# Four graph-attention layers on one Trainium2 core: the adjacency turned by DMA out of two bf16 scratch matrices in DRAM, in place of transposes on TensorE

## The chip, the cores and the metric

The kernel runs on one core of one Trainium2 chip. The metric is the device time of one execution in microseconds (us). Most executions of one kernel agree within 0.3%. The engines are called as the profile calls them: PE is TensorE (PEld its weight loads), DVE is VectorE, ACT is ScalarE, POOL is GpSimd and SP is SyncE. In the traces of this case ScalarE and PE are seen to take their instructions in the order in which the program lists them: in the changed kernel ScalarE stands 9.97 us at one instruction with a ready one behind it, and PE 5.88 us (both are shown below).

## The reference, cut to what matters

Sixteen batches, each a graph of 1024 nodes with 256 features, go through four attention layers one after the other. All four layers read the same adjacency matrix of the batch.

```python
x = normal(16, 1024, 256)                      # f32
a = bernoulli(1/256, (16, 1024, 1024))
a = a | swapaxes(a, -1, -2) | eye(1024)        # symmetric, with ones on the diagonal
adj = a.astype(int32)
# four times, with a different attention each time:
h = maximum(layernorm(x), 0)
x = x + attention_l(h, adj, W_l, a_l)          # [...]
```

The adjacency of one batch is 4 MB of int32. It is **symmetric** in these inputs.

## The kernel before

The kernel keeps a `mask` of uint8 in SBUF for each batch, with the neighbour on the partitions. The attention weights of a layer are a row (one value for each node, the same on all partitions), times or against a column value, times the mask. `load(b)` makes the mask: it fetches 128 rows of the adjacency (the DMA turns int32 into bf16), sums squares of them on ScalarE as a check that every entry is 0 or 1, turns the tile with eight TensorE transposes into PSUM, and casts it to uint8 on ScalarE.

```python
    def load(b):
        # [...] x_b, mask
        def fetch(i):
            fetched[i] = adjs.tile([P, N], BF, name="adj_i")          # adjs has 3 buffers
            nc.gpsimd.dma_start(fetched[i], adj[b, ts(i, P), :])       # L106
        for i in range(AHEAD):                                         # AHEAD = 2
            fetch(i)
        yield
        for i in range(NI):                                            # 8 tiles
            if i + AHEAD < NI:
                fetch(i + AHEAD)
            adj_i = fetched.pop(i)
            every = wide.tile([P, N], BF, name="wide")
            nc.scalar.activation(every, adj_i, AF.Square, bias=minus_half,
                                 accum_out=squares[:, b, i : i + 1])   # L117
            turned = psum.tile([P, NI, P], BF, name="misc", bufs=3)
            for j in range(NI):
                nc.tensor.transpose(turned[:, j, :], adj_i[:, ts(j, P)], ident_b)   # L122
            nc.scalar.copy(masks[b][:, :, ts(i, P)], turned)           # L123
            yield
```

Two streams of batches (even and odd) run interleaved. While layer 3 of batch b runs, `load(b + 2)` advances by one step for each half head:

```python
        coming = load(b + 2) if b + 2 < B else iter(())
        # [...] layers 0, 1 and 2
        yield from weigh3(0)                       # first row copy and weights of layer 3
        for n in range(H * NH):                    # 8 half heads
            yield from weigh3(n + 1)
            # [...] 8 matmuls accT <- V3, w        (L427)
            nc.scalar.copy(sums, accT)             # L431
            next(coming, None)                     # one step of load(b + 2)
```

The order in which this code is written is not the order in which the engines run it. A scheduler, working from its own idea of how long each instruction and each transfer takes, moves instructions forward on every engine. An instruction marked with `tc.keep_in_program_order` is exempt: it stays behind everything that was written before it for its engine. I call such an instruction *pinned*.

## Time and profile before

| | before |
|---|---|
| time, median of 3 runs | 3268.11 us (3267.7 to 3269.8) |
| span of the profiled execution, clock | 3267.0 us, 0.984 |
| PE busy, idle | 3075.9 us, 191.1 us |
| share of PE in the chain that ended last | 70% |

The prediction shows the lines for PE's fullness, for the transposes and for the start of layer 3. Two more views matter. The first is the page's part 4: the engines' shares of the chain of work that ended last, followed backwards from the last instruction.

```profile
PE 70%; DVE 18%; POOL 6%; issue 2%; ACT 2%; DMA 1%; SPq 0%; ACTq 0%; POOLq 0%
```

The second is the table of waits. A line names the engine, the tile and line that waited, after the arrow what it waited for, then us in total, how often, and the longest.

```profile
POOL adj_i L106 <- ACT sums L431: 214.6, 51, 14.8
DVE weights L262 <- ACT row L258: 84.6, 28, 8.6
```

The chain is mostly matmuls that follow one another.

### The profile page before, as it was taken

What the parts mean: (1) busy time and instruction counts of PE and PEld (TensorE: products, weight loads), DVE (VectorE), ACT (ScalarE), POOL (GpSimd) and SP (SyncE); (2) the same over time, 40 slices, a digit from 0 to 9 for tenths busy, and PEclk for the clock granted to TensorE, in tenths of its full rate; (3) what the DMA queues carried; (4) which work ended last, traced back from release to release, by engine and by line L of the source; (5) the groups of instructions that cost most, each with busy time, mean ns of one, the idle gap of its engine ahead of it and who ended that gap; (6) DMA issues with size and microseconds to landing.
All of it is one profiled execution on the core that took longest, in us unless ns stands there. A gap on an engine that the chain in (4) does not pass through costs nothing.

```text
span 3267.0 us, 38466 instructions
## 1 busy us (share of the span) xinstructions
PE 3075.9 (94%) x13702; PEld 2129.5 (65%) x13702; DVE 2546.5 (78%) x6140; ACT 969.5 (30%) x2081; POOL 1086.2 (33%) x1286
## 2 busy tenths in 40 slices
PE   6999999999999999999999999999999999999987
PEld 5776766657666676666766667676676766767562
DVE  5778787777877778877788877888778787787767
ACT  3423323232332323323233232322323223232121
POOL 1323424233242332423334233342323423233242
PEclk8999999999999999999999999999999999999998
DMA  4101101011010111100111010110101101000000
GB/s 118 27 4 17 33 12 41 7 16 30 14 39 7 17 29 17 36 10 13 30 17 36 10 17 28 15 36 13 39 4 17 33 13 40 4 14 13 1 13 14
DMA packets 55190, 73.18 MB, mean 22 GB/s; under 512 B 4048, under 2 KB 37968, under 8 KB 54992
## 3 DMA queue, kind: packets, MB, share of 16 engines
q0 software_dynamic: 18432, 33.56, 7.0%
q1 hardware_dynamic: 36560, 37.10, 3.6%
q8 instruction: 110, 1.80, 0.2%
q14 instruction: 88, 0.72, 0.1%
HBM read 87.43 MB, written 16.78 MB: 32 GB/s over the span
## 4 chain that ended last, share of the span: by engine, by line
PE 70%; DVE 18%; POOL 6%; issue 2%; ACT 2%; DMA 1%; SPq 0%; ACTq 0%; POOLq 0%
PE acc L346 31%; PE acc L427 22%; PE projected L242 11%; DVE weights L262 8%; PE misc L235 2%; PE misc L254 2%; POOL x_b L282 2%; DVE centered L227 2%; DVE stats L222 2%; POOL rstd L213 1%; PE misc L122 1%; DVE above L280 1%; DVE above L281 1%; DMA adj_i<-in_adj_dram 1%; POOL y L407 1%
## 5 line engine op out<-in xcount | busy, mean ns | idle before, releaser
L346 PE MATMUL acc<-V,weights 128*128 128x257 f32 x6144 | 1440.8, 384 | 8.4 <-DVE weights L262 7.0
L346 PEld LDWEIGHTS acc<-V,weights 128*128 128x128 f32 x6144 | 1139.5, 191 | 205.0 <-DVE weights L262 38.6
L427 PE MATMUL acc<-weights,V 128*65 128x512 f32 x2048 | 913.2, 594 | 0.3 <-DVE weights L262 0.3
L262 DVE SCALAR_TENSOR_TENSOR weights<-row,ex,mask 128x512 f32<-128x512 f32 x1024 | 744.9, 776 | 36.7 <-ACT row L258 36.7
L262 DVE SCALAR_TENSOR_TENSOR weights<-row,V,mask 128x512 f32<-128x512 f32 x768 | 593.4, 815 | 49.3 <-ACT row L258 47.9
L213 POOL TENSOR_TENSOR rstd<-rstd,minus_half 128x2 f32<-128x2 f32 (+1 forms) x320 | 330.2, 1034 | 883.3 <-DVE rstd L212 834.9
L427 PEld LDWEIGHTS acc<-weights,V 128*65 128x65 f32 x2048 | 279.4, 138 | 499.4 <-issue 477.2
L242 PE MATMUL projected<-W,hT 128*128 128x259 f32 (+1 forms) x2048 | 522.3, 397 | 40.8 <-DVE V L297 24.9
L242 PEld LDWEIGHTS projected<-W,hT 128*128 128x128 f32 x2048 | 388.1, 195 | 137.0 <-DVE V L297 37.5
L282 POOL TENSOR_TENSOR x_b<-x_b,above 128x256 f32<-128x256 f32 x256 | 222.1, 868 | 478.9 <-DVE above L281 436.6
L278 ACT ACTIVATE below<-acc,inv 128x256 f32<-128x256 f32 x256 | 121.0, 473 | 657.1 <-DVE inv L271 463.5
L222 DVE BATCH_NORM_STATS2 stats<-x_b 128x6 f32<-128x256 f32 x512 | 209.3, 415 | 126.0 <-POOL x_b L282 121.1
L235 PE MATMUL misc<-ident,centered 128*128 128x128 f32 x1024 | 168.5, 281 | 75.7 <-DVE centered L227 70.3
L237 ACT COPY hT<-misc 128x512 f32<-128x512 f32 x256 | 147.2, 588 | 299.6 <-PE misc L235 298.9
L227 DVE TENSOR_SCALAR centered<-x_b,mv 128x256 f32<-128x256 f32 x512 | 229.6, 451 | 4.7
L431 ACT COPY sums<-acc 65x512 f32<-65x512 f32 x128 | 74.1, 579 | 513.9 <-PE acc L427 512.4
L235 PEld LDWEIGHTS misc<-ident,centered 128*128 128x128 f32 x1024 | 120.8, 143 | 128.2 <-DVE centered L227 107.9
L258 ACT COPY row<-misc 128x512 f32<-128x512 f32 x224 | 129.8, 587 | 196.2 <-PE misc L254 196.0
L106 POOL DMA_DIRECT2D adj_i<-in_adj_dram x128 | 77.6, 606 | 287.4 <-ACT sums L431 214.6
L280 DVE TENSOR_SCALAR above<-acc,inv 128x256 f32<-128x256 f32 x256 | 122.8, 480 | 61.8 <-ACT below L278 60.9
L392 POOL TENSOR_TENSOR y<-y,bias 128x512 f32<-128x512 f32 x64 | 90.5, 1414 | 234.2 <-DVE y L439 215.9
L293 ACT ACTIVATE V<-projected,rstd 128x3 f32<-128x3 f32 x384 | 99.3, 263 | 228.0 <-PE projected L242 227.4
(70 smaller groups left out, 2311.4 us busy)
## 6 DMA issues: line engine op xcount, KB each, us to landing
adj_i<-in_adj_dram POOLq DMA_DIRECT2D x128, 256.0 KB, 3.9
x_b<-in_x_dram SPq DMA_DIRECT2D x16, 1024.0 KB, 7.9
out_dram<-y SPq DMA_DIRECT2D x32, 512.0 KB, 3.6
W<-in_L_gnn_W_dram SPq DMA_DIRECT2D x3, 256.0 KB, 3.6
a_b<-in_L_gnn_a_dram SPq DMA_DIRECT2D x3, 256.0 KB, 7.4
a_b<-in_L_gnn_a_src_dram SPq DMA_DIRECT2D x1, 640.0 KB, 8.4
a_b<-in_L_gnn_a_dst_dram SPq DMA_DIRECT2D x1, 640.0 KB, 10.2
W<-in_L_gnn_W_dram SPq DMA_DIRECT2D x2, 128.0 KB, 9.4
```

Source lines behind the costliest of these rows:

```text
L213: nc.gpsimd.tensor_tensor(r, r, minus_half.to_broadcast([P, n]), op=ALU.pow)
L222: nc.vector.bn_stats(stats, xb[:, 2 * pair + n, :])
L227: nc.vector.tensor_scalar(centered[:, n, :], xb[:, 2 * pair + n, :], mv[:, n, 0:1], 0.0, op0=ALU.subtract, op1=ALU.max,)
L235: nc.tensor.transpose(turned[:, k, ts(n, P)], centered[:, n, ts(k, P)], ident)
L237: nc.scalar.copy(hT, turned)
L242: nc.tensor.matmul(projected, hT[:, k, ts(n, P)], W[l][:, k, :], start=(k == 0), stop=(k == NK - 1),)
L258: nc.scalar.copy(r, turned)
L262: nc.vector.scalar_tensor_tensor(w[:, j, :], r, c(j), mask[:, j, ts(half, HALF)], op0=op, op1=ALU.mult)
L280: nc.vector.tensor_scalar(above, acc[:, :D], inv, 0.0, op0=ALU.mult, op1=ALU.max)
L282: nc.gpsimd.tensor_add(xi, xi, above)
L346: nc.tensor.matmul(acc, w[:, j, ts(i % NG, P)], V[:, j, : D + 1], start=(j == 0), stop=(j == NI - 1),)
L427: nc.tensor.matmul(accT, V3[:, j, h, :], w[:, j, :], start=(j == 0), stop=(j == NI - 1))
```

## The change

The intent is to take the 1024-element transposes of the adjacency off the full engine. For all batches but the first two, GpSimd issues four DMAs that copy the matrix, narrowed to bf16, into one of two scratch matrices in DRAM. SyncE then issues DMAs that read 128 columns of it and turn them on the way into SBUF. ScalarE casts the turned tile to the mask straight from SBUF. The four casting DMAs are pinned; the square and the mask cast, which read the turned tiles, are not.

```diff
+    dram = ctx.enter_context(tc.tile_pool(name="dram", bufs=1, space=bass.MemoryType.DRAM))
 [...]
+    narrows = [dram.tile([N, N], BF, name=f"narrow{n}") for n in range(2)]
 
     def load(b: int):
 [...]
+        by_dma = b >= 2
         fetched = {}
 
+        if by_dma:
+            for q in range(4):
+                rows = ts(q, N // 4)
+                cast = nc.gpsimd.dma_start(narrows[b % 2][rows, :], adj[b, rows, :])
+                tc.keep_in_program_order(cast)
+
         def fetch(i: int):
             fetched[i] = adjs.tile([P, N], BF, name="adj_i")
-            nc.gpsimd.dma_start(fetched[i], adj[b, ts(i, P), :])
+            if by_dma:
+                nc.sync.dma_start_transpose(fetched[i], narrows[b % 2][:, ts(i, P)])
+            else:
+                nc.gpsimd.dma_start(fetched[i], adj[b, ts(i, P), :])
 [...]
-            turned = psum.tile([P, NI, P], BF, name="misc", bufs=3)
-            for j in range(NI):
-                nc.tensor.transpose(turned[:, j, :], adj_i[:, ts(j, P)], ident_b)
-            nc.scalar.copy(masks[b][:, :, ts(i, P)], turned)
+            if by_dma:
+                nc.scalar.copy(masks[b][:, i, :], adj_i)
+            else:
+                # [...] as before
```

More of the change, by code (lines that the diff above doesn't have):

```diff
@@ L119, in load @@
             )
-            turned = psum.tile([P, NI, P], BF, name="misc", bufs=3)
-            for j in range(NI):
-                nc.tensor.transpose(turned[:, j, :], adj_i[:, ts(j, P)], ident_b)
-            nc.scalar.copy(masks[b][:, :, ts(i, P)], turned)
+            if by_dma:
+                nc.scalar.copy(masks[b][:, i, :], adj_i)
+            else:
+                turned = psum.tile([P, NI, P], BF, name="misc", bufs=3)
+                for j in range(NI):
+                    nc.tensor.transpose(turned[:, j, :], adj_i[:, ts(j, P)], ident_b)
+                nc.scalar.copy(masks[b][:, :, ts(i, P)], turned)
             yield
```

## The prediction

> **What bounds the kernel now.** I read the page's first two parts first: which engine is full, and whether it is full everywhere.
>
> ```profile
> PE 3075.9 (94%) x13702; PEld 2129.5 (65%) x13702; DVE 2546.5 (78%) x6140; ACT 969.5 (30%) x2081; POOL 1086.2 (33%) x1286
> PE   6999999999999999999999999999999999999987
> DMA  4101101011010111100111010110101101000000
> ```
>
> TensorE is busy in every slice; ScalarE and the DMA engines have most of their time free. So PE work that goes away is worth its full length, and work moved to ScalarE or the DMA engines costs nothing, as long as nobody on PE's path has to wait for it. Next come the groups of the adjacency (busy us, mean ns of one), and the chain of waits in a stretch where a tile is turned (start, us, what).
>
> ```profile
> L122 PE MATMUL misc<-ident_b,adj_i 128*128 128x128 bf16 x1024 | 80.9, 225 | 29.3 <-DVE ident_b L84 15.3 <-DMA adj_i<-in_adj_dram 12.3 <-ACT mask L123 1.2
> L123 ACT CAST mask<-misc 128x1024 uint8<-128x1024 bf16 x128 | 128.9, 1009 | 6.8 <-PE misc L122 6.8
> ...
> 1648.93 5.15 PE acc L427 x12
> 1654.08 0.45 PE misc L122 x8
> 1654.53 3.52 PE acc L346 x16
> ```
>
> One transpose lasts 225 ns but they are pipelined: eight of them, one adjacency tile, hold the chain for 0.45 us, between matmuls that follow without a gap. That is the price of a tile, not 8 x 225 ns. ScalarE waits only 6.8 us in all before the mask casts: the transposes it now depends on are never late.
>
> Last, what happens where layer 3 of a batch starts, since there the changed kernel does its casts. Timelines of three engines around 1600 us:
>
> ```profile
> 1599.48 0.73 POOL L321 TENSOR_TENSOR x_b<-x_b,beta 128x256 f32<-128x256 f32 x1
> ...
> 1605.97 1.08 ACT L237 COPY hT<-misc 128x512 f32<-128x512 f32 x2 [3.64 <-PE misc L235]
> 1609.24 0.58 ACT L258 COPY row<-misc 128x512 f32<-128x512 f32 x1
> ...
> 1612.64 1.92 PE L242 MATMUL projected<-W,hT 128*128 128x259 f32 x8
> 1614.40 7.03 PE L427 MATMUL acc<-weights,V 128*65 128x512 f32 x16
> ```
>
> From the last x_b + beta on GpSimd to the first layer-3 matmul are 14.9 us here. Over the 14 batches that load another, the timelines show two kinds: 14.9 us for odd batches, 11.2 us for even ones. The row copy on ScalarE must end before VectorE can make the weights (0.74 us each here), and those before L427.
>
> **What the Trainium skill says.** "DMA: Bandwidth & Descriptors", section "Anatomy of one DMA", fits a GpSimd-issued DMA as about 2.0 us fixed plus bytes at 436 GB/s. The trace agrees on the fixed part: an adjacency tile reads 512 KB and lands in 3.9 us. Its rate is lower: queue 0 wrote 33.56 MB in 7.0% of 3267 us = 229 us, so 147 GB/s written, 294 GB/s read.
>
> ```profile
> q0 software_dynamic: 18432, 33.56, 7.0%
> adj_i<-in_adj_dram POOLq DMA_DIRECT2D x128, 256.0 KB, 3.9
> ```
>
> The same page, "Latency and other measured facts", gives a DMA transpose an effective 261 GB/s for a non-contiguous case; "VectorE: DVE Perf Modes", section "The three transpose paths", gives 1309 ns for one 128x128 bf16 block. No transpose DMA is in this trace, so these stay unchecked. My estimate for one 128x1024 tile, from both: some 2 us fixed, 1 us of bytes, and the descriptors for eight blocks on top: 4.5 us to landing (3 to 10), and 2 us between tiles issued back to back. "TensorE: Matmul & The Clock Gate", Part 1, says that TensorE falls to half its clock after an idle window of about 3.4 us. The trace agrees: after PE had waited 2.0 us at 1522.8, the stretch that follows ran at a granted 0.58.
>
> ```profile
> 1505.00:1511.00 6.00, 6.00 (x15) 1.92 (x14) 6.00 (x10) 0.76 (x2) 2.38 (x2) 1.00 0.00 0
> 1522.70:1526.60 3.90, 3.80 (x7) 1.36 (x8) 3.87 (x21) 0.59 (x1) 2.54 (x4) 0.58 0.02 4
> ```
>
> 3.9 us at 0.58 instead of 1.00 lose 3.9 x 0.42 = 1.6 us.
>
> **The change part by part.**
>
> *Removed from PE.* 14 batches x 8 tiles = 112 of 128 groups of transposes: 112 x 0.45 = 50 us, all on the chain. With them go most of the waits they cause: PE's transposes of the sums wait 11.6 us for the mask cast, and GpSimd stands in front of tile fetches whose buffer isn't free. I put 12 us on these. Gain: 62 us.
>
> *ScalarE.* The mask cast now reads SBUF instead of PSUM, the same 1024 elements. The square over the same tile takes 1145 ns from SBUF, so I expect 1.0 to 1.15 us against 1009 ns: 0 to 16 us on an engine that is 30% busy. Nothing.
>
> *GpSimd.* 56 casts of a quarter (1 MB read, 0.5 MB written) replace 112 fetches at 606 ns. Nothing, and it no longer waits for buffers.
>
> *The new path: cast, transpose, square.* This is where I expect the cost. The instruction order of the changed kernel, which can be read without running it, has in every batch the same pattern. On GpSimd the four casts stand right behind the last x_b + beta, with two tiles' V products between them. On ScalarE the first square of the new tile stands behind the hT copies of the last pair, **ahead of** the first row copy of layer 3. ScalarE takes its instructions in order. The square needs the first transpose, which needs all four casts. Before, the tile had been fetched long ahead; now the scheduler puts some 8 us between cast and square.
>
> Worked for an odd batch on the clock above. Casts issue from 1600.2 (end of x_b + beta) to about 1604. 4 MB at 294 GB/s are 14.3 us; with about 2 us of start and completion they end near 1617. The first transpose lands 4.5 us later, at 1621. ScalarE stands at the square from 1607. After it come the square (1.33 us with its accumulator read), one or two ex and h copies (0.75), the row copy (0.58), and one weights instruction (0.74): L427 starts at about 1621 + 3.4 = 1624.4 instead of 1614.4, 10 us late. PE can't fill this: in its order L427 stands before the other stream's matmuls. For an even batch the room is 11.2 instead of 14.9 us: 13.6 us late. Mean 11.8.
>
> After a gap of such length PE runs some 4 us at about half clock: 1.6 us. Later in the batch three casts into the mask follow soon after the square that frees their transpose's buffer (three buffers): ScalarE stands again for about 4.5 - 3 us each time. PE has queued work then, so I count 2 us per batch. Sum: 11.8 + 1.6 + 2 = 15.4 us, x 14 = 216 us.
>
> *Net.* 3268 - 62 + 216 = 3422. Large descriptors could make the casts somewhat faster than the fetches' 294 GB/s, so I go down a little: 3400.
>
> **The rivals.** (1) *The DMA path is hidden and only the 62 us show: 3206.* For it: the DMA engines are nearly idle, a batch takes 200 us, and eight tiles at 4.5 us need 36. Against it: what counts is not the rate but the distance between the casts and the first square in program order, and that is 8 us where at least 10 of cast and 3 of transpose have to fit, even at the best rate. With 10 us of cast and 3 of transpose, L427 is still 3 to 7 us late: 14 x (5 + 3) - 62 = +50, 3318. (2) *The transposes are slow, 10 us each and one after the other.* Nothing in this trace speaks against it. Then tile 0 comes 5.5 us later, and the second and third, which stand before the second row copy, hold ScalarE again by some 5 to 10 us: 14 x 28 - 62 = +330, 3600. (3) *The casts from DRAM to DRAM are slower than the fetches,* because they write to DRAM: 20 instead of 14.3 us adds 14 x 6 = 80 us: 3480. (4) *The new order of instructions happens to be better or worse elsewhere.* The scheduler rearranges around it; the pattern is the same in all batches, so a few us per batch either way, +-40.
>
> **Range and chances.** Rival 1's milder form (3318) and rival 3 to halfway rival 2 (3480 to 3560) set the range: 3290 to 3560. Faster by over 2% means below 3203, more than the whole gain of 62 us without any cost: 0.04. Within 2%, up to 3333, needs less than 9 us lost per batch: 0.16. Slower: 0.80.
>
> **What would show it.** Right: the chain of waits has no L122 group in later batches; ScalarE's square idles for 9 to 20 us once per batch, released by the DMA of adj_i; the first L427 of each batch stands about 25 us behind the last x_b + beta, and the window behind it has a granted clock near 0.6; the issues list gives casts of about 14 us for a batch and transposes of 3 to 6 us to landing; busy time of PE falls by about 50 us while its idle time rises by 150 or more. Wrong: if the squares wait little, my clock of the casts is off (they issue earlier or move faster than 294 GB/s); if ScalarE waits as long as I say and the time hardly grows, PE had other work in its queue; if the waits lie at the mask casts and not at the square, it is the transposes that are slow.

## More of the kernel before

GpSimd stands for 214.6 us in front of fetches of adjacency tiles, and nobody is seen to suffer from it: in the whole run ScalarE's squares wait 8.2 us for fetched tiles. VectorE waits 84.6 us for the row copies on ScalarE.

## The result, and the profile after

| | before | after |
|---|---|---|
| time, median (range), 4 runs each in the same rounds | 3268.29 us (3267.7 to 3269.8) | 3392.74 us (3389.9 to 3400.36) |
| span of the profiled execution, clock | 3267.0 us, 0.984 | 3388.3 us, 0.973 |
| PE busy, idle | 3075.9, 191.1 us | 3045.9, 342.4 us |

The ratio is 1.0379, with a 95% interval of 1.0363 to 1.0395. Ratios in this document are the mean time of one kernel's fast runs over the mean of the other's fast runs of the same rounds, so they are not quite the ratio of the medians beside them. The results are correct. The changed kernel is 3.8% slower.

The added lines of code shift the line numbers. In the changed kernel the square is L129, the mask cast from SBUF L133, the row copy L273 (L258 before), the transposes that make a row L269 (L254), the weights L277 (L262), and the layer-3 matmul L442 (L427).

From the page of the changed kernel, parts 1, 2 and 4: busy time of each engine, busy tenths of PE and DMA in 40 slices, and the engines' shares of the last chain.

```profile
PE 3045.9 (90%) x12806; PEld 2091.9 (62%) x12806; DVE 2551.7 (75%) x6140; ACT 969.7 (29%) x2081; POOL 1048.9 (31%) x1230
...
PE   6989899898998989989899898998999888999987
...
DMA  4110210202002020020201102020020211200000
...
PE 44%; DVE 37%; POOL 8%; DMA 6%; ACT 3%; issue 2%; SPq 0%; ACTq 0%; POOLq 0%
```

PE has lost 30 us of work and gained 151 us of idle time (342.4 against 191.1). Its row of solid nines has broken into eights and nines: the loss is spread over the whole run. DMA, 1% of the chain before, now has 6%.

The page's parts 3 and 6 say how the new transfers went: the queue of the casting DMAs (packets, MB, share of 16 engines' time), then the issues with their size and the median us from issue to landing.

```profile
q0 software_dynamic: 4096, 33.56, 5.1%
...
narrow<-in_adj_dram POOLq DMA_DIRECT2D x56, 512.0 KB, 8.1
...
adj_i<-narrow SPq DMA_TRANSPOSE x112, 3.5
```

A transposing DMA lands after 3.5 us in the median (3.1 to 5.4 over all). The transfers are not slow. The waits tell who stood for them:

```profile
DVE weights L277 <- ACT row L273: 244.7, 27, 16.1
...
ACT wide L129 <- DMA adj_i<-narrow: 159.2, 14, 13.2
...
PE misc L269 <- ACT ex L328: 111.5, 14, 10.5
...
ACT mask L133 <- DMA adj_i<-narrow: 53.5, 50, 3.3
```

The second line carries the result: ScalarE's square waits 14 times, once for each batch loaded in the new way, 11.4 us on average. The waits of VectorE for ScalarE's row copies have grown from 84.6 to 244.7 us with it, and PE waits 14 times for `ex`, which ScalarE makes too. The chain of waits in one such place shows the path (start, us, what):

```profile
1660.09 0.72 POOL x_b L336
1660.81 0.55 POOL narrow L110
...
1664.65 9.38 DMA narrow<-in_adj_dram
...
1674.17 3.43 DMA adj_i<-narrow
...
1677.63 0.02 ACT wide L129
...
1679.60 0.47 PE misc L269
1680.08 3.41 PE projected L257 x8
1683.48 6.87 PE acc L442 x16
```

This is the same batch whose start of layer 3 the prediction shows at 1600 us. The casts are issued right behind the last x_b + beta, the last of the four lands at 1674.05, the first turned tile 3.4 us after its issue, and only then does ScalarE go on. The timelines of ScalarE and PE in the same stretch show what stood behind the square (start, us, engine, line, operation; in brackets the idle time before it and what ended it):

```profile
1666.58 1.08 ACT L252 COPY hT<-misc 128x512 f32<-128x512 f32 x2 [3.64 <-PE misc L250]
1677.63 1.15 ACT L129 ACTIVATE wide<-adj_i,minus_half 128x1024 bf16<-128x1024 bf16 x1 [9.97 <-DMA adj_i<-narrow]
...
1679.79 0.60 ACT L273 COPY row<-misc 128x512 f32<-128x512 f32 x1
1680.25 2.97 ACT L133 CAST mask<-adj_i 128x1024 uint8<-128x1024 bf16 x3
...
1679.08 1.00 PE L269 MATMUL misc<-ident,ex 128*128 128x128 f32 x2 [5.88 <-ACT ex L328]
...
1683.32 7.03 PE L442 MATMUL acc<-weights,V 128*65 128x512 f32 x16
```

ScalarE stood for 9.97 us with the `ex` and the row copy queued behind the square, although PE had finished the projection that this `ex` reads at 1669.3. From the start of the last x_b + beta (1660.09) to the first layer-3 matmul (1683.32) are 23.2 us; before, in the same batch, 14.9 us. PE stood for 5.88 us, from 1673.2 to 1679.08, at the transposes of `ex` that make a row, with eight projection matmuls (`projected`) queued behind them; the last part of this wait and the work after it fall into a window at half the clock, in which the eight took 3.61 us in place of 1.92. In the chain these eight, and not the row copy or the weights, stand last before the layer-3 matmul. Columns of the windows: start and end, length, busy time of PE, PEld, DVE, ACT and POOL, granted clock, DMA share, GB/s.

```profile
1677.00:1683.00 6.00, 3.87 (x10) 2.92 (x11) 2.58 (x4) 5.37 (x10) 1.49 (x4) 0.50 0.50 93
```

I read the start of layer 3 off the timelines in all batches, and split the time into this *stage* (last x_b + beta to first layer-3 matmul) and the rest of the batch:

| | before | after |
|---|---|---|
| stage, even batches (start to start) | 11.2 us | 22.5 to 23.7 us |
| stage, odd batches | 14.9 us | 22.5 to 23.7 us |
| stages of the 14 batches that load another, sum of the increase | | +142 us |
| rest of these batches, sum | 2618 us | 2599 us, so -19 us |
| start of the run and its tail | | -5 us |

The sum, +118 us, is the difference of the two spans (+121) to within what such reading gives. The stages are longer by 10.15 us each, and the rest is shorter by only 1.3 us. PE's own waits give nearly the same: it waits 111.5 us for `ex`, 8.0 us per batch, where the kernel before has no such wait on PE, and the half clock from there to the layer-3 matmul costs 1.9 us per batch by the trace.

### The profile page after: what moved, and what is told of

The parts are those of the page before. It is cut to its first block, busy times and chain, and to the rows that moved or that the text cites. A ratio compares the mean times of both kernels' runs of the same rounds, so it can differ in the third digit from the quotient of the medians.

```text
span 3388.3 us, 36818 instructions
## 1 busy us (share of the span) xinstructions
PE 3045.9 (90%) x12806; PEld 2091.9 (62%) x12806; DVE 2551.7 (75%) x6140; ACT 969.7 (29%) x2081; POOL 1048.9 (31%) x1230
## 2 busy tenths in 40 slices
DMA packets 159121, 102.45 MB, mean 30 GB/s; under 512 B 121425, under 2 KB 155345, under 8 KB 158033
## 3 DMA queue, kind: packets, MB, share of 16 engines
q1 hardware_dynamic: 154832, 66.47, 8.0%
## 4 chain that ended last, share of the span: by engine, by line
PE 44%; DVE 37%; POOL 8%; DMA 6%; ACT 3%; issue 2%; SPq 0%; ACTq 0%; POOLq 0%
PE acc L361 20%; DVE weights L277 18%; PE acc L442 14%; PE projected L257 7%; DMA narrow<-in_adj_dram 4%; DVE centered L242 3%; DVE stats L237 2%; POOL x_b L297 2%; POOL y L407 2%; DVE above L295 2%; DMA adj_i<-narrow 2%; PE misc L250 2%; DVE y L408 1%; DVE V L312 1%; DVE above L296 1%
## 5 line engine op out<-in xcount | busy, mean ns | idle before, releaser
L361 PE MATMUL acc<-V,weights 128*128 128x257 f32 x6144 | 1423.1, 381 | 7.5 <-DVE weights L277 5.3
L442 PE MATMUL acc<-weights,V 128*65 128x512 f32 x2048 | 922.5, 599 | 0.3 <-DVE weights L277 0.3
L277 DVE SCALAR_TENSOR_TENSOR weights<-row,ex,mask 128x512 f32<-128x512 f32 x1024 | 745.4, 775 | 199.2 <-ACT row L273 199.2
L277 DVE SCALAR_TENSOR_TENSOR weights<-row,V,mask 128x512 f32<-128x512 f32 x768 | 582.7, 801 | 47.6 <-ACT row L273 45.5
L442 PEld LDWEIGHTS acc<-weights,V 128*65 128x65 f32 x2048 | 283.1, 140 | 507.4 <-issue 488.0
L257 PE MATMUL projected<-W,hT 128*128 128x259 f32 (+1 forms) x2048 | 543.0, 409 | 52.1 <-DVE V L312 24.5
L257 PEld LDWEIGHTS projected<-W,hT 128*128 128x128 f32 x2048 | 397.5, 201 | 164.3 <-ACT hT L252 53.7
L242 DVE TENSOR_SCALAR centered<-x_b,mv 128x256 f32<-128x256 f32 x512 | 247.0, 485 | 4.3
L250 PEld LDWEIGHTS misc<-ident,centered 128*128 128x128 f32 x1024 | 120.4, 142 | 180.7 <-DVE centered L242 134.8
L129 ACT ACTIVATE wide<-adj_i,minus_half 128x1024 bf16<-128x1024 bf16 x128 | 146.1, 1144 | 168.8 <-DMA adj_i<-narrow 159.2
L269 PE MATMUL misc<-ident,ex 128*128 128x128 f32 x512 | 89.2, 283 | 112.1 <-ACT ex L328 111.5
L273 ACT COPY row<-misc 128x512 f32<-128x512 f32 x224 | 129.9, 587 | 144.2 <-PE misc L269 144.1
```

Source lines behind the costliest of these rows:

```text
L242: nc.vector.tensor_scalar(centered[:, n, :], xb[:, 2 * pair + n, :], mv[:, n, 0:1], 0.0, op0=ALU.subtract, op1=ALU.max,)
L250: nc.tensor.transpose(turned[:, k, ts(n, P)], centered[:, n, ts(k, P)], ident)
L257: nc.tensor.matmul(projected, hT[:, k, ts(n, P)], W[l][:, k, :], start=(k == 0), stop=(k == NK - 1),)
L277: nc.vector.scalar_tensor_tensor(w[:, j, :], r, c(j), mask[:, j, ts(half, HALF)], op0=op, op1=ALU.mult)
L361: nc.tensor.matmul(acc, w[:, j, ts(i % NG, P)], V[:, j, : D + 1], start=(j == 0), stop=(j == NI - 1),)
L442: nc.tensor.matmul(accT, V3[:, j, h, :], w[:, j, :], start=(j == 0), stop=(j == NI - 1))
```

## The experiments

My theory was: the loss is the distance in ScalarE's order between the casts and the first reader of a turned tile, and nothing else about the DMA path costs anything. The rivals were: the turning DMAs themselves are dear, or their many small packets disturb others (the trace counts 121,425 packets under 512 B, against 4,048 before); the casts from DRAM to DRAM take bandwidth; the transposes taken off PE were never worth the 62 us. Ten kernels ran, in three calls, each with three rounds beside the kernel before. All ten gave correct results. The ones that do not turn the tiles are correct only because the adjacency is symmetric.

| run | what differs | time, median | ratio to before (95%) |
|---|---|---|---|
| e1_readers_pinned | after, readers pinned | 3220.78 | 0.985 (0.9834 to 0.9867) |
| e2_casts_early | after, casts issued some layers earlier | 3239.65 | 0.991 (0.9888 to 0.9931) |
| e3_rows_not_turned | after, plain DMA in place of the turning one | 3429.94 | 1.0495 (1.0477 to 1.0512) |
| e5_no_turn | before, without the transposes | 3289.5 | 1.0056 (1.0039 to 1.0073) |
| e8_before_pinned | before, readers pinned | 3259.47 | 0.997 (0.9953 to 0.9987) |
| e5_no_turn_pinned | e5_no_turn, readers pinned | 3230.42 | 0.9882 (0.9866 to 0.9899) |
| e1_square_pinned | after, only the square pinned | 3381.78 | 1.0354 (1.0335 to 1.0374) |
| e4_unpinned | after, casts not pinned | 3269.36 | 0.9999 (0.9983 to 1.0016) |
| e7_early_and_pinned | e2 with readers pinned | 3227.39 | 0.9865 (0.9849 to 0.9882) |
| e9_readers_pinned_casts_free | e1 with casts not pinned | 3250.85 | 0.9939 (0.9922 to 0.9956) |

The kernel before gave medians of 3270.74 (beside the first four), 3268.86 (beside the next four) and 3270.16 us (beside the last two). Seven runs stand behind each of these medians. A difference between kernels of different calls is uncertain by the 2 us or so by which these differ.

### Pin the readers (e1_readers_pinned)

```diff
-            nc.scalar.activation(
+            sq = nc.scalar.activation(
                 every, adj_i, AF.Square, bias=minus_half, accum_out=squares[:, b, i : i + 1]
             )
             if by_dma:
-                nc.scalar.copy(masks[b][:, i, :], adj_i)
+                tc.keep_in_program_order(sq)
+            if by_dma:
+                tc.keep_in_program_order(nc.scalar.copy(masks[b][:, i, :], adj_i))
```

> Only the two ScalarE instructions that read the turned tile (square, mask cast) are pinned behind what was traced before them on ScalarE, so the first one stands behind the second sums copy of layer 3 instead of ahead of the first row copy; casts and transposes stay where they are. My theory (the cost is the distance in ScalarE's order between casts and first reader): the wait of the square for the transposed tile falls from 159 us to under 20, the distance from the last x_b + beta to the first layer-3 matmul goes back from 22.5 to 10.5 and 14.2 us, and the time falls by about 14 x 10 = 140 us, to 3225 to 3260. Rival (the DMA work itself, contention or slow transposes, costs): the time stays above 3340.

Measured: 3220.78 us (3218.69 to 3224.29). That is 1.5% below the kernel before, 4 us below the expected range, and 172 us below the changed kernel, with the same transfers in number and size (102.45 MB in both). The timelines of this kernel in the same batch (here the row copy is L275, the sums copy L448, the layer-3 matmul L444):

```profile
1573.67 0.72 POOL L338 TENSOR_TENSOR x_b<-x_b,beta 128x256 f32<-128x256 f32 x1
1574.34 1.18 POOL L110 DMA_DIRECT2D narrow<-in_adj_dram  x2
...
1583.43 0.58 ACT L275 COPY row<-misc 128x512 f32<-128x512 f32 x1
...
1588.58 7.03 PE L444 MATMUL acc<-weights,V 128*65 128x512 f32 x16
...
1612.32 0.58 ACT L448 COPY sums<-acc 65x512 f32<-65x512 f32 x1 [6.60 <-PE acc L444]
1612.80 1.15 ACT L129 ACTIVATE wide<-adj_i,minus_half 128x1024 bf16<-128x1024 bf16 x1
```

The casts are issued just where they are in the changed kernel, right behind the last x_b + beta. What moved is the reader: the first square now stands behind the second sums copy, 38 us after the first cast's issue, and finds its tile ready. The row copy has nobody in front of it, and the layer-3 matmul stands 14.9 us behind the x_b + beta, as in the kernel before. No square or mask cast waits for a turned tile anywhere in the trace. The theory holds: where the readers stand is worth the whole loss and more. Of the 172 us, 142 are the stages and 31 the rest of the 14 batches. One reservation: the pins also make the scheduler shift other instructions. Compared by operation and tile name in the traces, 98 of the 1697 ScalarE instructions beside the readers stand at another place in the order than in the changed kernel. The next run comes nearer to a single cause.

### Issue the casts earlier (e2_casts_early)

```diff
         V = yield from attend(0, V, finish0, 1)
+        if b + 2 < B:
+            narrow(b + 2)          # the four casts, moved here out of load(), still pinned
         V = yield from attend(1, V, finish, 2)
```

(the comment is not in the code; the lines that left `load()` are not shown)

> The casts are issued earlier, after layer 0 of the batch, some 80 us ahead of layer 3; nothing is pinned on ScalarE, so the scheduler may also move the readers up. My theory, if the readers keep their place: as in e1, 3225 to 3260. If the scheduler puts the first reader again just behind the moment at which it believes the tile landed, the wait moves with it, and the time is between 3260 and 3390. Rival (the DMA work itself): above 3340.

Measured: 3239.65 us (3235.18 to 3249.2), the second way to open the distance, from its other end, and inside the first expected range. The stages are back at those of the kernel before. The free readers have moved with the casts, but hardly anything else has: 12 of 1697 other ScalarE instructions and 56 of 12,678 matmuls stand elsewhere than in the changed kernel. What keeps it behind e1 is in part that the readers are still free: mask casts wait 62.2 us for turned tiles, in 51 short waits of up to 2.8 us, and e7 below, which pins them, is 12 us faster.

### A plain DMA in place of the turning one (e3_rows_not_turned)

```diff
-                nc.sync.dma_start_transpose(fetched[i], narrows[b % 2][:, ts(i, P)])
+                nc.sync.dma_start(fetched[i], narrows[b % 2][ts(i, P), :])
```

> The transposing DMA is replaced by a plain load of rows from the same scratch matrix (right here only because the inputs' adjacency is symmetric). Casts and order stay. My theory (most of the wait is the casts, a transpose lands in 3.5 us): a plain load lands perhaps 0.5 to 1 us earlier, so 3370 to 3390. Rival (turning by DMA is what is slow): the wait mostly goes and the time is under 3320.

Measured: 3429.94 us (3424.76 to 3436.67). Both expectations missed: a transfer that lands sooner (2.9 us against 3.5) made the kernel 37 us slower. Its waits:

```profile
ACT wide L129 <- DMA adj_i<-narrow: 188.3, 14, 15.3
PE projected L257 <- ACT hT L252: 170.3, 32, 12.5
```

I had not looked at the order of this kernel before it ran. In that order the scheduler, which seems to reckon a plain load shorter than a turning one (the traces don't show its reckoning), has put the square and two mask casts another step forward than in the changed kernel, in front of the hT copies of the last pair. Now PE's projection waits for hT as well, and the stage takes 25.2 to 27.5 us from the end of x_b + beta (21.8 to 23.0 in the changed kernel, 10.5 and 14.2 before). As a test of the turning this run failed, since it changed two things at once. It agrees with the theory, though it doesn't isolate it: the faster transfer loses where its reader stands earlier.

### Take the transposes away, and nothing else (e5_no_turn)

```diff
-            turned = psum.tile([P, NI, P], BF, name="misc", bufs=3)
-            for j in range(NI):
-                nc.tensor.transpose(turned[:, j, :], adj_i[:, ts(j, P)], ident_b)
-            nc.scalar.copy(masks[b][:, :, ts(i, P)], turned)
+            if b >= 2:
+                nc.scalar.copy(masks[b][:, i, :], adj_i)
+            else:
+                # [...] as before
```

> The kernel before, without the transposes on TensorE in the last 14 batches and with nothing in their place: the mask is cast straight from the fetched tile (right here only because the adjacency is symmetric). No scratch, no extra DMA. It measures the gain that the change could have had. My prediction's term: 3268 - 62 = 3206. The trace after hints at less, since outside the stage where layer 3 starts a batch became only 1.3 us shorter: then 3268 - 14 x 1.3 = 3250. I expect 3205 to 3250.

Measured: 3289.5 us (3287.39 to 3295.62), so removing 112 groups of transposes without any new transfer makes the kernel before slower. The expectation missed for the same reason as in e3:

```profile
ACT mask L121 <- DMA adj_i<-in_adj_dram: 180.7, 102, 4.5
```

The transposes on PE had been a brake: the mask cast could not be put before them. Without them the scheduler moves the cast up, presumably to where it believes the tile has landed, and it waits there 102 times. A kernel with something removed is not a measure of what was removed, if the scheduler is free to rearrange the rest. So the next two runs pin the readers in both.

### The same comparison with the readers pinned (e8_before_pinned, e5_no_turn_pinned)

Both pin the square and the mask cast for batches from 2 on, as e1 does; e8 in the kernel before (shown), the other in e5_no_turn.

```diff
+            if b >= 2:
+                tc.keep_in_program_order(sq)
 [...]
+                tc.keep_in_program_order(cast)
```

> The kernel before, TensorE transposes and all, with only its two ScalarE readers of the adjacency (square, mask cast) pinned in program order from batch 2 on. It asks whether the pins alone give what e1 gained (3271 to 3221). My theory (e1's 50 us are the transposes that left TensorE): no change, 3255 to 3285. Rival (the pins are the gain): about 3220 to 3235.

> e5 again with the two readers pinned. In e5 the mask casts waited 181 us for their tile's DMA, because the scheduler had moved them up. My theory: with the pins these waits go, and what is left is the kernel before without the 112 groups of transposes: 3271 less 50 to 62, 3205 to 3225, so the same as e1 within 10 us, which would mean that the whole DMA path of e1 costs nothing. Rival (taking the transposes away doesn't help because VectorE bounds those stretches): 3250 to 3290.

Measured: 3259.47 us (3258.62 to 3259.74) and 3230.42 us (3230.23 to 3231.25). The first lies in its expected range; the second missed, 5 us above its own and below the rival's. The pins alone give the kernel before 9 us; why was not followed up (in the traces VectorE's waits for row copies fall from 84.6 to 46.2 us). Without the transposes it is 29 us faster again, and the 180.7 us of mask-cast waits are gone. That is 0.26 us for each of the 112 groups, in place of the 0.45 that each holds on the chain. From e8 to e5_no_turn_pinned PE's busy time falls by 47 us in the profiles (3072.5 to 3025.3), but its idle time grows by 18 (185.2 to 203.3): part of what is removed comes back as waiting. The pins don't hold everything: 826 of 12,678 other matmuls and 91 of 1697 other ScalarE instructions stand at another place in the two orders, so the 29 us are the removal and what the scheduler made of it. The comparison of e5_no_turn_pinned with e1 is cleaner. PE, VectorE and ScalarE have the same order in both, instruction by instruction; only GpSimd and the transfers differ. e1 with its casts and turns is 10 us faster, so its path costs nothing. Why it is even faster stays open. In e5_no_turn_pinned GpSimd stands 274.8 us in front of fetches whose buffer a mask cast still holds, and in e1 there are no such fetches; that is a plausible reading, not a tested one. e7, which has the same order on these three engines and no such fetches either, gains only 3 us.

### Pin only the square (e1_square_pinned)

```diff
             if by_dma:
                 tc.keep_in_program_order(sq)
             if by_dma:
-                tc.keep_in_program_order(nc.scalar.copy(masks[b][:, i, :], adj_i))
+                nc.scalar.copy(masks[b][:, i, :], adj_i)
```

(shown against e1)

> Only the square is pinned. In the instruction order the first mask cast then takes the square's old place on ScalarE, between the ex copies of the last pair. My theory: the wait passes to the mask cast, the distance from the last x_b + beta to the first layer-3 matmul stays above 21 us, and the time stays at 3370 to 3410. Rival (something particular to the square, as its 1.3 us in that place): a gain of over 60 us.

Measured: 3381.78 us (3377.85 to 3391.84), nearly the changed kernel's time. The wait has gone to the next reader:

```profile
ACT mask L135 <- DMA adj_i<-narrow: 206.8, 57, 13.1
```

The first mask cast of each batch now stands where the square stood. The longest wait, 13.1 us, is about that of the square in the changed kernel (13.2). It is not the square that costs; it is whatever reader of the new tile comes first in ScalarE's order.

### Unpin the casts (e4_unpinned)

```diff
                 cast = nc.gpsimd.dma_start(narrows[b % 2][rows, :], adj[b, rows, :])
-                tc.keep_in_program_order(cast)
```

> The change without its pins on the casts: the scheduler lets the casts go about half a batch earlier on GpSimd, and moves the first mask casts of a tile up too. As in e2, the casts then have time, and only small waits of the mask casts for single transposes stay: 3235 to 3265, so the pins on the casts are what makes the change slow. If the order of the casts doesn't matter: 3390.

Measured: 3269.36 us (3267.97 to 3272.09), equal to the kernel before and slightly above the expected range. The scheduler moves the free casts far forward, and the stages are as before. Two things remain that can account for this: mask casts wait 62.4 us in 49 short waits, and the run starts later. The first layer-3 matmul of the run stands at 219.4 us, against 204.3 in the kernel before. The casts of the first two batches loaded in the new way are now issued at the very start, beside the first fetches: between 30 and 100 us the DMA engines' share is 0.39 in place of 0.15, and PE is busy 52.5 us in place of 65.8.

### Early casts with pinned readers (e7_early_and_pinned)

This is e2 with both pins of e1; the diff is the sum of theirs.

> e2 and e1 together: casts early, readers pinned. e1 had no wait for the transposed tiles left, so an earlier cast has nothing to remove: 3215 to 3228, the same as e1. If something of the casts still costs in e1 (their traffic or their place on GpSimd at the start of layer 3), this is 10 us or more faster than e1.

Measured: 3227.39 us (3225.03 to 3228.01). Earlier casts give nothing more once the readers are placed; the ratio, 0.9865, lies within the interval of e1. PE, VectorE and ScalarE have the order of e1, instruction by instruction. So the casts' traffic and place at the start of layer 3 are no second cost in e1.

### Pinned readers with free casts (e9_readers_pinned_casts_free)

This is e1 with the diff of e4.

> e1 without the pins on the casts. If the readers' place is all that matters, the casts' pins are no longer needed: 3215 to 3235. In e4 the free casts of the first loaded batches ran at the very start beside the first fetches and cost TensorE some 16 us there; if that stays, 3230 to 3245.

Measured: 3250.85 us (3248.68 to 3252.65), slightly outside both expected ranges and 30 us slower than e1. Half of it is the late start again (first layer-3 matmul at 218.6 us, against 204.1 in e1). The other half, 15 us over the batches, goes with this:

```profile
POOL narrow L110 <- DMA adj_i<-narrow: 114.5, 11, 11.4
```

GpSimd now meets the casts so early that the scratch matrix is still being read by the turning DMAs of the earlier batch that used it, and it stands in front of them, with its other work behind. So the pins that the change put on the casts were useful. What it lacked were pins on the readers.

The fastest of all, e1_readers_pinned, beats both kernels.

## Why the prediction was right

The prediction said 3400 us, in a range of 3290 to 3560, and slower by over 2%. Measured were 3392.74 us and +3.8%. It was right, and by the mechanism that it named. Two of its terms were mis-sized, the gain and the cost, and since their errors partly cancel, it is luck that 3400 came within 8 us.

**The bound.** TensorE is full in every slice, as read. But the step "PE work that goes away is worth its full length" is where the gain came out too large. The prediction put 50 us on the transposes and 12 us on their waits, 62 in all. With the readers pinned in both, the removal is worth 29 us (e5_no_turn_pinned beside e8_before_pinned), and 39 us with the new path in place of the fetches (e1 beside e8). The 50 us between e1 and the kernel before hold the 9 us of the pins as well. In the changed kernel itself only 19 us were realised in the rest of the batches, and PE's busy time fell by 30 us where the prediction had about 50; some 27 us of matmul time at half clock (14 x 1.9, an estimate) hide the difference.

**ScalarE's mask cast from SBUF.** Expected at 1.0 to 1.15 us; it took 1.05 (1.01 from PSUM). The cost was nothing, as said.

**GpSimd.** Right: its waits in front of the fetches of batches from 2 on, most of 214.6 us, went away and gave nothing that can be told apart.

**The new path.** The distance in program order was the cost, as predicted: one wait of the square for each of 14 batches, with work behind it that PE needs. e1, which pins the readers, and e2, which issues the casts earlier, show it: with the same transfers both bring the stages back to 11.2 and 14.9 us. The path behind the square was not quite the predicted one. PE doesn't stop at the layer-3 matmul for want of weights; it stops before that, at the transposes of `ex` that make a row, and then has eight projections to run at half clock. So from the square to the layer-3 matmul it took 5.4 us in the mean, where the prediction had 3.4 by way of the row copy and the weights. The size was off in the other direction. The prediction had the casts end 17 us after the last x_b + beta and the turned tile land 4.5 us later. The trace has 13.3 us from the first cast's issue (1660.76) to the last landing (1674.05), and 3.4 us for the tile: about 17 us from issue to square in place of 20.8. With the slow clock the stage was predicted 13.4 us longer (11.8 + 1.6); it was 10.15 us longer (11.8 in even batches, 8.5 in odd ones, where the prediction had 13.6 + 1.6 and 10 + 1.6). Over 14 batches that is 46 us, and it is the term of the sum that was too large.

**The slow clock.** Right in size: 1.9 us per batch in place of 1.6. They sit within the 10.15 us. One reading was wrong: the prediction says that the trace agrees with an idle window of about 3.4 us, but the wait that it shows is 2.0 us, so this place shows the half clock and not that window.

**The later mask-cast waits.** Predicted 2 us per batch. In the rest of a batch e1 gains 3.5 us over the kernel before (49 us over 14), and the changed kernel 1.3. The difference, 2.2 us per batch, is in e1 gone together with the 53.5 us of mask-cast waits. This fits, although e1 pins both readers at once and so does not separate it from other effects of the order.

**The sum.** The wrong order costs 172 us in all (the changed kernel beside e1), where the prediction had 216. The gain was 50 with the pins in place of 62. The errors, 44 too much cost and 12 too much gain, partly cancel, and the last 22 us were taken off by a guess (3422 to 3400). That 3268 - 50 + 172 gives 3390 is no test, since both figures come from e1.

**The rivals.** The first, a hidden path, is false for the order as it was, and nearly true once the order is mended: e1 at 3220.78 us is 15 us above its 3206, and 9 of its 50 us are what the pins gave the kernel before. The second and the third, slow turns and slow casts, fall by the landings themselves (3.5 and 8.1 us) and by e1, which has the same transfers and is the fastest. The fourth, other effects of a new order, was given +-40 us. No run isolates it in the changed kernel; in another one, with no new transfer at all, the pins alone move e5_no_turn by 59 us (3289.5 to 3230.42).

## What to carry to other kernels

When a scheduler places the reader of a DMA by its own idea of when the data lands, and the engine takes its instructions in order, one reader that stands too early holds everything behind it; so when an operation moves to a DMA, read the new order on the engine that consumes the result and pin *all* its readers behind work that covers the real landing, since a wait that is taken from one reader passes to the next. Removing an operation can also remove the brake that kept a later one in place, so measure what a removal is worth with the order of the rest held as fixed as can be, and compare the orders: pins on two readers left others free to move. And place a transfer as late as its distance to the reader allows: issued as soon as possible, it ran into the start of the program and into the previous readers of its scratch.

## What the Trainium skill lacked or had wrong

- "DMA: Bandwidth & Descriptors", section "Latency and other measured facts", has only rates for a transposing DMA, 261 GB/s in a non-contiguous case and about 350 to 400 in a contiguous one, and the 1309 ns that the prediction cites are for one 128x128 block. For one tile of 128x1024 bf16 (256 KB) the trace shows what a kernel needs to know: 3.5 us from issue to landing in the median (3.1 to 5.4), and 1.17 us of issue on SyncE. The rate was lower here: queue 1 carries 29.4 MB more than before (66.47 against 37.10), for 8.0% of 3388.3 us against 3.6% of 3267.0, which is 153 us more, so some 191 GB/s (an estimate: other transfers of this queue can have slowed too).
- "TensorE: Matmul & The Clock Gate", Part 1, ties the half clock to an idle window of about 3.4 us. In the changed kernel the trace agrees: in a wait of 5.88 us (1673.2 to 1679.08) the clock fell, and it was 0.50 from 1677 to 1683. But in the kernel before a wait of 2.0 us was enough for 0.58 in the 3.9 us that follow. A plan that counts only on gaps above 3.4 us would miss these. The page also tells of short idles that bring the half clock on, but gives no length for them.
- No page that I read says that the reader of a DMA, placed too early in an engine's program, holds the work behind it, or that a wait taken from one reader passes to the next. Here it was 172 us of 3393, most of it in 14 waits with a mean of 11.4 us, and pinning the readers mended it with the same transfers.
